# Layer two's feed-forward part: fifteen taps of a third tile on VectorE, joined on TensorE by an identity; means subtracted from PSUM; the residual projection at the head of a strip's tail

## The chip, the cores and the metric

The kernel runs on one core of one Trainium2 chip. The metric is the device time of one execution in microseconds, the median of several runs. A profiled execution is a separate one, and its own time is given beside them.

## The reference, cut to what matters

The network has four layers over four images of 64x64 tokens with 96 channels. The selective scans of the first two take the first 12030 us of the profile's 15132. The change touches only the feed-forward part of the second layer. Its input `y` has 192 channels, it works on 768 hidden channels (`HID`), and it ends in 96:

```python
def msffn(y, in_w, in_b, dw1, dw3, dw5, ln_g, ln_b, out_w, out_b):
    hcl = jax.nn.silu(y @ in_w.T + in_b)
    hc = hcl.transpose(0, 3, 1, 2)
    hc = hc + dwconv(hc, dw1) + dwconv(hc, dw3) + dwconv(hc, dw5)
    hn = layernorm(hc.transpose(0, 2, 3, 1), ln_g, ln_b)
    return hn @ out_w.T + out_b
```

`dwconv` is a convolution with one filter per channel over the 64x64 image. The three of them and the identity are folded into one 5x5 filter of 25 taps. Beside this the layer adds the projection of `y` to 96 channels and the residual `x`, with a skip factor.

## The kernel before

The 768 hidden channels are six tiles of 128 partitions, numbered 0 to 5. The tokens are eight strips of 32 image rows (2048 tokens, four chunks of 512). For one strip and one tile the kernel

- zeroes a padded image `pad` of 36x68 on GpSimd (L1657), makes the hidden values with TensorE into PSUM tile `c` (L1666; four pieces of 512 tokens and a remainder of 128, two halves of the 192 channels each), and writes silu of it into `pad` on ScalarE (L1674). Tiles `ON_PE = (0, 2, 3, 5)` use `padp` (two buffers), tiles 1 and 4 use `padv` (one buffer);
- convolves. For the tiles on TensorE (`on_pe`), each tap is 16 matmuls with a diagonal 32x32 weight, at 16 positions of the array (L1697), added up in four PSUM banks `d0` to `d3`, of which there is one set. ScalarE copies them out in 16 pieces into `hcp` (L1712). For tiles 1 and 4 (`on_dve`) VectorE does one multiply (L1731) and 24 multiply-adds (L1733) over the whole strip, in `hcv`.

When a strip's six tiles are there, `leave` ends the strip, which is called its tail here: TensorE adds the channels up into the mean (`average`, L1743; the four chunks at the four column positions of the array), ScalarE copies it out (L1765), TensorE spreads it over the partitions chunk by chunk (L1770), ScalarE copies that to `means` (L1774), VectorE subtracts it from each of the six tiles (L1778), ScalarE squares them (L1750, a thread of its own, at most two ahead), TensorE averages the squares (L1743), ScalarE and VectorE make the reciprocal deviation (L1793, L1795). Then, for each chunk: spread it (L1799), copy it (L1809), project `y` (L1814), add to the residual `x` (L1818), six output matmuls (L1823), two VectorE operations (L1825, L1827), and a store (L1828). PSUM tile `m`, used for everything that is spread, projected or put out, has one buffer. The residual `x` is loaded at L1783, in the middle of the tail.

Each engine runs its instructions in the order in which they were issued. That order is set by the class `Plan`. Every step of work is a Python generator (a thread: `loads`, `leave`, `enter` for either group of tiles, `on_pe`, `on_dve`). It names an engine and a duration (`yield "PE", 5.3`) before it issues, or a condition that it waits for. `Plan.run` keeps a time for every engine, always takes the thread that could start soonest, and after each step lets it go on 0.2 us later. So the durations written in the code decide how threads are interleaved. `loads` issues a strip's `y` load (L1642, 1632 KB) once the strip two before it is `done`, as its buffer is one of two.

Of the kernel before, what the change touches and what calls it, by code (L numbers as in the profile page):

```python
# [211 lines left out]
class Plan:  # L212
# [3 lines left out]
    def __init__(self, fill=None):  # L216
        self.threads, self.free, self.fill, self.current = [], {}, fill, None
# [20 lines left out]
    def run(self):  # L238
        now = 0.0
        while self.threads:  # L240
# [20 lines left out]
            th.wants = next(th.work, None)  # L261
            if th.wants is None:
                self.threads.remove(th)
# [1310 lines left out]
def layer1_ffn(k, a, x_in, y_in, x_out):  # L1574
# [5 lines left out]
    with ExitStack() as ctx:  # L1580
# [23 lines left out]
        ON_PE = (0, 2, 3, 5)  # L1604
        taps = k.load(w, a["L1_dw5"], "taps")
# [26 lines left out]
        plan, held = Plan(), {"c": 0}  # L1632
        for st in strips:
            st.lo, st.hi = max(0, st.r0 - 2), min(HW, st.r0 + ROWS + 2)
            st.y, st.pads, st.hc, st.ready, st.done = None, {}, {}, set(), False
        old = lambda st, n: st.n < n or strips[st.n - n].done

        def loads():
            for st in strips:
                yield lambda: old(st, 2)  # L1640
                st.y = k.t(io, [C, 2, (ROWS + 4) * HW], "y")
                nc.sync.dma_start(  # L1642
                    st.y[:, :, : (st.hi - st.lo) * HW],
                    y_in[:, st.b, st.lo * HW : st.hi * HW].rearrange("(h c) t -> c h t", c=C),
                )
                yield "DMA", 10.0
# [36 lines left out]
        def on_pe():  # L1683
            for st in strips:
                for t in ON_PE:
                    yield lambda: st.pads.get(t) is not None
                    pad = st.pads[t]

                    pc = [k.t(psd, [128, CH], f"d{i}") for i in range(4)]
                    for tap in range(25):  # L1690
                        if tap % 5 == 0:
                            yield "PE", 5.3
                        dy, dx = divmod(tap, 5)
                        for i in range(4):
                            mine = slice(i * 32, (i + 1) * 32)
                            for j in range(4):
                                nc.tensor.matmul(  # L1697
                                    pc[i][j * 32 : (j + 1) * 32, :],
                                    diag[mine, ON_PE.index(t), tap, :],
                                    pad[mine, j * 8 + dy : j * 8 + dy + 8, dx : dx + HW],  # L1700
                                    start=tap == 0,
                                    stop=tap == 24,
# [4 lines left out]
                    yield lambda: st.n == 0 or ON_PE.index(t) < 2 or strips[st.n - 1].done  # L1707
                    hc = k.t(io, [128, ROWS * HW], "hcp", bufs=6)
# [8 lines left out]

        def on_dve():
            for st in strips:
                for t in ON_DVE:  # L1720
                    yield lambda: st.pads.get(t) is not None
                    pad = st.pads[t]
                    yield lambda: st.n == 0 or t == ON_DVE[0] or strips[st.n - 1].done
                    hc = k.t(io, [128, ROWS * HW], "hcv", bufs=3)
                    to = hc.rearrange("p (r w) -> p r w", w=HW)
                    for tap in range(25):
                        yield "DVE", 2.35
                        dy, dx = divmod(tap, 5)
                        win, wt = pad[:, dy : dy + ROWS, dx : dx + HW], taps[:, t, tap : tap + 1]
                        if tap == 0:  # L1730
                            nc.vector.tensor_scalar_mul(to, win, wt)  # L1731
                        else:
                            nc.vector.scalar_tensor_tensor(to, win, wt, to, op0=ALU.mult, op1=ALU.add)  # L1733
# [7 lines left out]
        def average(ps, v, first, last):  # L1741
            for at, cols in chunks:
                nc.tensor.matmul(ps[at, :], avg, v[:, cols], start=first, stop=last, tile_position=(0, at.start))  # L1743

        def squares(st):
            for t in st.order:
                yield lambda: t in st.centred and len(st.squared) - st.summed < 2
                sq = k.t(work, [128, ROWS * HW], "sq", bufs=2)
                yield "ACT", 1.9
                nc.scalar.activation(sq, st.hc[t], AF.Square)  # L1750
                st.squared.append(sq)

        def leave():
            for st in strips:
                st.order, st.centred, st.squared, st.summed = [], set(), [], 0
                mean = k.t(psm, [128, CH], "s")
                while len(st.order) < NT:
# [3 lines left out]
                    yield "PE", 1.0  # L1761
# [4 lines left out]
                means = k.t(work, [128, ROWS * HW], "means", bufs=1)  # L1766
                for at, cols in chunks:
# [5 lines left out]
                    yield "ACT", 0.6  # L1773
                    nc.scalar.copy(means[:, cols], p)  # L1774
                plan.add(squares(st))
                for t in st.order:
                    yield "DVE", 2.3
                    nc.vector.tensor_sub(st.hc[t], st.hc[t], means)  # L1778
                    st.centred.add(t)
                xs = []  # L1780
                for at, cols in chunks:
                    x = k.t(work, [C, CH], "x", bufs=4)
                    nc.sync.dma_start(x, x_in[:, st.b, st.r0 * HW + cols.start : st.r0 * HW + cols.stop])  # L1783
                    xs.append(x)
                var = k.t(psm, [128, CH], "s")
                for n in range(NT):
                    yield lambda: len(st.squared) > n
                    yield "PE", 1.0
                    average(var, st.squared[n], n == 0, n == NT - 1)
# [6 lines left out]
                for j, (quarter, cols) in enumerate(chunks):  # L1796
# [13 lines left out]
                    pp = k.t(ps, [C, CH], "m")  # L1810
                    at = (st.r0 - st.lo) * HW + j * CH
                    yield "PE", 1.8
                    for half in range(2):
                        nc.tensor.matmul(  # L1814
# [664 lines left out]
```

## Time and profile before

| what | us |
|---|---|
| runs, median of 3 | 15260.64 (15258.76 to 15286.69) |
| profiled execution, its own time | 15133.75 |
| span of the profile | 15131.9 |
| the stage: first c matmul, end of strip 0, end of strip 6, last VectorE operation | 12049.8, 12422.8, 13813.6, 13965.8 |
| one strip in the middle, from y load to y load | 231.5 to 232.0 |

The span runs from the first to the last instruction of the execution. A line of the groups reads: line, engine, operation, output and input by the program's names, shapes, count | busy time, mean ns of one | idle time of the engine ahead of them and what ended it. A line of the waits reads: who <- whom: us in total, times, longest. A line of a timeline reads: start, duration, engine, line, operation, names, shapes, count of records, and the idle time ahead in brackets; a matmul of 32-bit numbers shows as two records. "The granted clock" is the share of TensorE's full clock that the chip let through.

### The profile page before, as it was taken

To read this page: it belongs to the slowest core of one execution; us is meant where nothing else is said; L and a number is where in the kernel's file an instruction comes from. 1 tells how busy PE (TensorE), PEld (TensorE's weight loads), DVE (VectorE), ACT (ScalarE), POOL (GpSimd) and SP (SyncE) were. 2 spreads that over 40 slices of the span, in tenths; PEclk is the share of its full clock that TensorE was granted. 3 is DMA by queue.
4 is the path that set the end of the run, shared out by engine and by line. 5 is a ranking of instruction groups with operands and counts; after the bars stand their busy time and mean duration, and the time that the engine had idled before them with its cause. 6 is when DMAs were issued, how large, how long until landed. Compare 5 with 4: busy or idle time off the path is not lost. (4 is left out here: it accounts for less than half of the span.)

```text
span 15131.9 us, 190905 instructions
## 1 busy us (share of the span) xinstructions
PE 13534.7 (89%) x71561; PEld 4825.7 (32%) x71561; DVE 12601.9 (83%) x9389; ACT 8242.6 (54%) x13165; POOL 9773.6 (65%) x4913
## 2 busy tenths in 40 slices
PE   8899899989998999899989998998899889898877
PEld 3232323232323232322222223222222244443344
DVE  1999799979997999799979997999999855565655
ACT  3666466656665666466656665665566333332333
POOL 0788688868886888688858885887788600000123
PEclk9899899989998999899989998999899899998888
DMA  2333433343334333445455445445545400000122
GB/s 69 120 122 118 160 115 124 117 156 124 115 126 147 126 113 127 160 158 165 159 164 167 160 149 177 162 151 163 174 156 165 140 11 12 18 19 17 48 72 71
DMA packets 713945, 1821.70 MB, mean 120 GB/s; under 512 B 108966, under 2 KB 274603, under 8 KB 709244
## 3 DMA queue, kind: packets, MB, share of 16 engines
q1 hardware_dynamic: 676156, 1733.94, 35.5%
q0 software_dynamic: 36864, 75.55, 1.7%
q8 instruction: 566, 9.27, 0.3%
q14 instruction: 359, 2.94, 0.1%
HBM read 1429.25 MB, written 379.91 MB: 120 GB/s over the span
## 5 line engine op out<-in xcount | busy, mean ns | idle before, releaser
L1155 POOL TENSOR_TENSOR hc<-h,bc 128x1024 f32<-128x1024 f32 x2304 | 5413.4, 2364 | 769.7 <-DVE h L1135 706.0
L1135 DVE TENSOR_TENSOR_SCAN h<-da,state,t 128x1024 f32<-128x1024 f32 x2112 | 4836.4, 2327 | 3.1 <-ACT da L1124 3.1
L1128 DVE TENSOR_TENSOR t<-u,bc 128x1024 f32<-128x1024 f32 x2816 | 3309.2, 1216 | 280.1 <-PE u L1116 198.5
L1124 ACT ACTIVATE da<-dts,L_A_logs 128x1024 f32<-128x1024 f32 x2816 | 3188.1, 1146 | 597.0 <-DVE h L1135 562.6
L1164 PE MATMUL y<-hc,gather_y 128*32 128x512 f32 x9216 | 2807.7, 643 | 44.7 <-POOL hc L1155 44.5
L1155 POOL TENSOR_TENSOR area<-h,bc 128x1024 f32<-128x1024 f32 x768 | 1813.8, 2362 | 652.7 <-DVE h L1135 593.8
L1116 PE MATMUL u<-dtu,spread 32*128 32x512 f32 x3072 | 1705.9, 679 | 416.4 <-DVE t L1128 406.8
L1135 DVE TENSOR_TENSOR_SCAN h<-da,t 128x1024 f32<-128x1024 f32 x704 | 1569.8, 2266 | 16.7 <-ACT da L1124 8.8
L1182 PE MATMUL y<-L_diag,zeros 96*32 96x256 f32 x5024 | 1263.0, 388 | 0.0
L1050 ACT COPY dt<-m 96x512 f32<-96x512 f32 x512 | 297.2, 580 | 1355.2 <-PE m L1047 1354.5
L1164 PE MATMUL y<-area,gather_y 128*32 128x512 f32 x3072 | 1005.1, 739 | 5.1 <-ACT yc L1193 3.6
L1116 PEld LDWEIGHTS u<-dtu,spread 32*128 32x128 f32 x3072 | 546.2, 197 | 1405.3 <-issue 948.7
L1164 PEld LDWEIGHTS y<-hc,gather_y 128*32 128x32 f32 x9216 | 523.6, 115 | 1379.6 <-issue 953.0
L1657 POOL MEMSET padp<- 128x2448 f32 x32 | 68.4, 2139 | 1385.8 <-PE d L1697 1368.3
L1733 DVE SCALAR_TENSOR_TENSOR hcv<-padv,taps,hcv 128x2048 f32<-128x2048 f32 x384 | 902.2, 2349 | 13.4
L1697 PE MATMUL d<-padp,diag 32*32 32x512 f32 x25600 | 885.7, 601 | 2.0 <-ACT hcp L1712 2.0
L1182 PEld LDWEIGHTS y<-L_diag,zeros 96*32 96x32 f32 x5024 | 522.6, 112 | 811.9 <-issue 458.3
L1107 POOL TENSOR_TENSOR area<-area,bc 128x1024 f32<-128x1024 f32 x256 | 603.3, 2357 | 172.7 <-DMA area<-u_dram 172.7
L963 PE MATMUL m<-xs,proj 96*128 96x512 f32 (+1 forms) x1024 | 553.2, 649 | 86.8 <-ACT spare L1209 39.7
L963 PE MATMUL m<-area,proj 96*128 96x512 f32 (+1 forms) x1024 | 549.9, 648 | 88.7 <-ACT dt L978 41.0
L1047 PE MATMUL m<-dtu,ident 96*96 96x512 f32 x1024 | 582.8, 652 | 24.9 <-ACT xs L937 12.4
L1697 PEld LDWEIGHTS d<-padp,diag 32*32 32x32 f32 x25600 | 482.7, 103 | 371.4 <-issue 196.9
(289 smaller groups left out, 18174.1 us busy)
## 6 DMA issues: line engine op xcount, KB each, us to landing
bc<-bc_dram SPq DMA_DIRECT2D x1024, 512.0 KB
dts<-dt_dram SPq DMA_DIRECT2D x768, 512.0 KB
area<-u_dram SPq DMA_DIRECT2D x256, 512.0 KB
dt_dram<-dt SPq DMA_DIRECT2D x256, 384.0 KB
y_tok<-spare SPq DMA_DIRECT2D x64, 768.0 KB
dt<-y_tok SPq DMA_DIRECT2D x128, 384.0 KB
u_dram<-dtu SPq DMA_DIRECT2D x128, 384.0 KB
x_tok<-area SPq DMA_DIRECT2D x32, 768.0 KB
```

Of the source, the lines that this page charges most:

```text
L963: nc.tensor.matmul(v.ps, seg.proj[:, src, to], seg.xs[:, src, chunks[j]], start=src == 0, stop=src == 1)
L1047: nc.tensor.matmul(v.ps, k.ident[:C, :C], term[:, half, chunks[j]], start=at == 0, stop=at == 3)
L1107: self.nc.gpsimd.tensor_mul(gr.t, gr.u, self.bc[:, 0, gr.sg, :])
L1116: self.nc.tensor.matmul(seg.u[:, cols], self.spread[rows, :], seg.dtu[rows, half, cols], start=True, stop=True)
L1124: self.nc.scalar.activation(gr.da, gr.seg.dts[gr.cb], AF.Exp, scale=scale)
L1128: self.nc.vector.tensor_mul(gr.t, gr.seg.u, self.bc[:, 0, gr.sg, :])
L1135: self.nc.vector.tensor_tensor_scan(gr.h[:, order], gr.da[:, order], gr.t[:, order], start, op0=ALU.mult, op1=ALU.add)
L1155: self.nc.gpsimd.tensor_mul(gr.hc, gr.h, self.bc[:, 1, gr.sg, :])
L1164: nc.tensor.matmul(seg.y[at : at + GC, :], self.gather_y, gr.hc[:, part * CH : (part + 1) * CH], start=gr.sg == 0, stop=gr.sg == NSG - 1, ...
L1182: self.nc.tensor.matmul(gr.seg.y[at : at + GC, :256], self.zeros, gr.seg.bt.lay.diag.rearrange("p h t c -> p (h t c)")[:, :256], start=Fal ...
L1697: nc.tensor.matmul(pc[i][j * 32 : (j + 1) * 32, :], diag[mine, ON_PE.index(t), tap, :], pad[mine, j * 8 + dy : j * 8 + dy + 8, dx : dx + H ...
L1733: nc.vector.scalar_tensor_tensor(to, win, wt, to, op0=ALU.mult, op1=ALU.add)
```

## The change

- Tile 3 (`SHARED`) is convolved by two engines: TensorE does its taps 0 to 9 (`ROWS_PE = 2` rows of five), VectorE does taps 10 to 24 into the tile's own `hcp` buffer, and TensorE adds that buffer to the four PSUM banks by 16 matmuls with a 32x32 identity. VectorE takes the tiles in the order 1, 3, 4.
- The spread mean isn't copied to `means`: VectorE subtracts it from PSUM, chunk by chunk (24 operations in place of six). The squares and their averages go in two halves of 1024 tokens.
- The load of `x`, the four projections of `y` and the adding to `x` come first in `leave`, before the means.
- `padp` has three buffers instead of two, `hcp` seven instead of six; `Plan(tight=True)` leaves the 0.2 us out when a thread's next step is on the same engine; some of the durations named in the code change. The threads `leave` and `squares` get precedence at equal times, and the buffer of `y` is two rows smaller (the loads are as they were).

```diff
             th.at = start + us + (0.2 if us else 0.0)
             th.wants = next(th.work, None)
+            if self.tight and isinstance(th.wants, tuple) and th.wants[0] == engine:
+                th.at -= 0.2
...
         ON_PE = (0, 2, 3, 5)
+        SHARED, ROWS_PE = ON_PE[2], 2
...
-        plan, held = Plan(), {"c": 0}
+        plan, held = Plan(tight=True), {"c": 0}
...
-                st.y = k.t(io, [C, 2, (ROWS + 4) * HW], "y")
+                st.y = k.t(io, [C, 2, (ROWS + 2) * HW], "y")
...
+                    hc = None
+                    if t == SHARED:
+                        hc = st.share = k.t(io, [128, ROWS * HW], "hcp", bufs=7)
+                    last = ROWS_PE * 5 if t == SHARED else 24
                     pc = [k.t(psd, [128, CH], f"d{i}") for i in range(4)]
-                    for tap in range(25):
-                        if tap % 5 == 0:
-                            yield "PE", 5.3
+                    for tap in range(last + 1):
+                        if tap % 5 == 0 and tap < 25:
+                            if t == SHARED and tap == last:
+                                yield lambda: st.shared
+                                yield "PE", 1.1
+                            else:
+                                yield "PE", 5.3
                         dy, dx = divmod(tap, 5)
                         for i in range(4):
                             mine = slice(i * 32, (i + 1) * 32)
                             for j in range(4):
+                                whole = t == SHARED and tap == last
                                 nc.tensor.matmul(
                                     pc[i][j * 32 : (j + 1) * 32, :],
-                                    diag[mine, ON_PE.index(t), tap, :],
-                                    pad[mine, j * 8 + dy : j * 8 + dy + 8, dx : dx + HW],
+                                    eye[mine, :] if whole else diag[mine, ON_PE.index(t), tap, :],
+                                    hc[mine, j * CH : (j + 1) * CH]
+                                    if whole
+                                    else pad[mine, j * 8 + dy : j * 8 + dy + 8, dx : dx + HW],
                                     start=tap == 0,
-                                    stop=tap == 24,
+                                    stop=tap == last,
...
-                    yield lambda: st.n == 0 or ON_PE.index(t) < 2 or strips[st.n - 1].done
-                    hc = k.t(io, [128, ROWS * HW], "hcp", bufs=6)
+                    if hc is None:
+                        yield lambda: st.n == 0 or t in ON_PE[:2] or strips[st.n - 1].done
+                        hc = k.t(io, [128, ROWS * HW], "hcp", bufs=7)
...
+        def convolve(pad, t, hc, first):
+            to = hc.rearrange("p (r w) -> p r w", w=HW)
+            for tap in range(first, 25):
+                yield "DVE", 1.3 if tap == first else 2.35
+                dy, dx = divmod(tap, 5)
+                win, wt = pad[:, dy : dy + ROWS, dx : dx + HW], taps[:, t, tap : tap + 1]
+                if tap == first:
+                    nc.vector.tensor_scalar_mul(to, win, wt)
+                else:
+                    nc.vector.scalar_tensor_tensor(to, win, wt, to, op0=ALU.mult, op1=ALU.add)
+
         def on_dve():
             for st in strips:
-                for t in ON_DVE:
+                for t in (ON_DVE[0], SHARED, ON_DVE[1]):
+                    if t == SHARED:
+                        yield lambda: st.share is not None
+                        yield from convolve(st.pads[t], t, st.share, ROWS_PE * 5)
+                        st.shared = True
+                        continue
...
                     yield lambda: st.n == 0 or t == ON_DVE[0] or strips[st.n - 1].done
                     hc = k.t(io, [128, ROWS * HW], "hcv", bufs=3)
-                    to = hc.rearrange("p (r w) -> p r w", w=HW)
-                    for tap in range(25):
...
+                    yield from convolve(st.pads[t], t, hc, 0)
                     st.pads[t] = None
...
+        def average(ps, v, first, last, part=chunks):
+            start = part[0][1].start
+            for at, cols in part:
+                mine = v[:, cols.start - start : cols.stop - start]
+                nc.tensor.matmul(ps[at, :], avg, mine, start=first, stop=last, tile_position=(0, at.start))
...
         def squares(st):
-            for t in st.order:
-                yield lambda: t in st.centred and len(st.squared) - st.summed < 2
-                sq = k.t(work, [128, ROWS * HW], "sq", bufs=2)
-                yield "ACT", 1.9
...
+            for half in range(2):
+                for t in st.order:
+                    yield lambda: st.centred > half and len(st.squared) - st.summed < 2
+                    sq = k.t(work, [128, ROWS * HW // 2], "sq", bufs=2)
+                    yield "ACT", 1.05
+                    nc.scalar.activation(sq, st.hc[t][:, half * 2 * CH : (half + 1) * 2 * CH], AF.Square)
+                    st.squared.append(sq)
...
         def leave():
             for st in strips:
-                st.order, st.centred, st.squared, st.summed = [], set(), [], 0
-                mean = k.t(psm, [128, CH], "s")
+                st.order, st.centred, st.squared, st.summed = [], 0, [], 0
+                mean, xs = k.t(psm, [128, CH], "s"), []
+                yield lambda: st.y is not None
+                for at, cols in chunks:
+                    x = k.t(work, [C, CH], "x", bufs=4)
+                    nc.sync.dma_start(x, x_in[:, st.b, st.r0 * HW + cols.start : st.r0 * HW + cols.stop])
+                    xs.append(x)
+                for j in range(4):
+                    pp = k.t(ps, [C, CH], "m")
+                    at = (st.r0 - st.lo) * HW + j * CH
+                    yield "PE", 1.8
+                    for half in range(2):
+                        nc.tensor.matmul(
+                            pp, proj_w[:, half, :], st.y[:, half, at : at + CH], start=half == 0, stop=half == 1
+                        )
+                    yield "DVE", 0.75
+                    nc.vector.scalar_tensor_tensor(xs[j], xs[j], cb, pp, op0=ALU.add, op1=ALU.add)
                 while len(st.order) < NT:
                     yield lambda: st.ready - set(st.order)
                     t = min(st.ready - set(st.order))
                     st.order.append(t)
-                    yield "PE", 1.0
+                    yield "PE", 1.4
                     average(mean, st.hc[t], len(st.order) == 1, len(st.order) == NT)
                 yield "ACT", 0.6
...
-                means = k.t(work, [128, ROWS * HW], "means", bufs=1)
-                for at, cols in chunks:
+                plan.add(squares(st), 1)
+                for j, (at, cols) in enumerate(chunks):
                     yield "PE", 0.9
                     p = k.t(ps, [128, CH], "m")
                     nc.tensor.matmul(
...
-                    yield "ACT", 0.6
-                    nc.scalar.copy(means[:, cols], p)
-                plan.add(squares(st))
-                for t in st.order:
-                    yield "DVE", 2.3
-                    nc.vector.tensor_sub(st.hc[t], st.hc[t], means)
-                    st.centred.add(t)
-                xs = []
-                for at, cols in chunks:
-                    x = k.t(work, [C, CH], "x", bufs=4)
-                    nc.sync.dma_start(x, x_in[:, st.b, st.r0 * HW + cols.start : st.r0 * HW + cols.stop])
-                    xs.append(x)
+                    yield "DVE", 3.8
+                    for t in st.order:
+                        nc.vector.tensor_sub(st.hc[t][:, cols], st.hc[t][:, cols], p)
+                    st.centred = (j + 1) // 2
...
-                for n in range(NT):
+                for n in range(2 * NT):
                     yield lambda: len(st.squared) > n
-                    yield "PE", 1.0
-                    average(var, st.squared[n], n == 0, n == NT - 1)
+                    yield "PE", 0.7
+                    half, at = divmod(n, NT)
+                    average(var, st.squared[n], at == 0, at == NT - 1, chunks[2 * half : 2 * half + 2])
                     st.summed += 1
...
                     nc.scalar.copy(rs, p)
-                    pp = k.t(ps, [C, CH], "m")
...
-                    yield "DVE", 0.7
-                    nc.vector.scalar_tensor_tensor(xs[j], xs[j], cb, pp, op0=ALU.add, op1=ALU.add)
                     po = k.t(ps, [C, CH], "m")
...
-        plan.add(leave())
-        plan.add(enter(ON_PE, "padp", 2))
+        plan.add(leave(), 1)
+        plan.add(enter(ON_PE, "padp", 3))
```

## The prediction, made before the result was known

> **What bounds the kernel now.** I read the utilisation by slice first, for where the changed stage lies (12038 to 13966 us of the span of 15131.9), then one steady strip of it through the windows view, the groups, the waits and the timelines, and last the end of the stage.
>
> The windows view of a strip (us, then each engine's busy time, granted clock, DMA share, GB/s):
>
> ```profile
> 12666.40:12897.90 231.50, 212.23 (x3496) 95.74 (x3496) 140.05 (x69) 74.69 (x112) 12.83 (x6) 0.96 0.07 16
> ```
>
> TensorE is busy 212 of 231.5 us, VectorE 140, ScalarE 75: TensorE bounds the strip, and VectorE has about 90 us of room. Six such periods, 231.8 each, lie between the end of strip 0 and the end of strip 6. The groups of the strip (busy, mean ns | idle before, releaser) and its waits:
>
> ```profile
> L1733 DVE SCALAR_TENSOR_TENSOR hcv<-padv,taps,hcv 128x2048 f32<-128x2048 f32 x48 | 112.8, 2349 | 1.7
> L1697 PE MATMUL d<-padp,diag 32*32 32x512 f32 x3200 | 111.0, 600 | 0.0
> L1778 DVE TENSOR_TENSOR hcp<-hcp,means 128x2048 f32<-128x2048 f32 x4 | 9.0, 2285 | 45.4 <-ACT means L1774 45.4
> L1825 DVE TENSOR_TENSOR rs<-rs,m 96x512 f32<-96x512 f32 x4 | 2.7, 684 | 21.8 <-PE m L1823 21.8
> ```
> ```profile
> PE c L1666 <- DMA y<-y: 12.5, 1, 12.5
> PE s L1743 <- ACT hcp L1712: 6.2, 2, 4.4
> ```
>
> The taps are over half of TensorE's work. Its idle time is 19.4 us: 12.5 for the y load, 6.2 for ScalarE's copies out of PSUM, 0.8 small. The timeline shows prices and what follows a wait:
>
> ```profile
> 12666.47 3.75 PE L1666 MATMUL c<-y,in_w 96*128 96x512 f32 x4 [12.48 <-DMA y<-y]
> ...
> 12672.35 1.98 PE L1666 MATMUL c<-y,in_w 96*128 96x512 f32 x4
> ...
> 12681.75 5.55 PE L1697 MATMUL d<-padp,diag 32*32 32x512 f32 x160
> ...
> 12721.27 3.72 PE L1743 MATMUL s<-hcp,avg 128*32 128x512 f32 x8 [4.43 <-ACT hcp L1712]
> ...
> 12783.98 1.06 PE L1743 MATMUL s<-sq,avg 128*32 128x512 f32 x8
> ```
>
> Start to start, five taps cost 5.49, a c pair 1.91 (0.64 for the 2-row remainder), an averaging call 1.0, a row spread 1.04, a projection 1.8, six output matmuls 5.2. The strip is then 20x5.49 + 24x1.91 + 6x0.64 + 12x1.0 + 8x1.04 + 4x1.8 + 4x5.2 = 208; with 19.4 idle 227; the other 4 are the slow instructions behind a wait (3.75 for 1.98, 3.72 for 1.06).
>
> **The change on TensorE, by strip.** Tile 3 keeps 10 of its 25 taps: three groups of five go, -16.5. The identity adds 16 matmuls of the taps' own shape, 16/80 of a group: +1.1. The averages of squares become 12 calls with two column positions instead of 6 with four. No row shows such a call. Two passes of one position follow each other, and a whole-width pass takes 1.91/4 = 0.48, so two positions cost 0.96, as much as four do now; if the price went by count it would be 0.5. I take 1.0, +6 (bounds 0 and +6). Work: 208 - 16.5 + 1.1 + 6 = 198.6.
>
> **VectorE, by strip.** The shared tile adds one multiply (1.28) and 14 taps at a pitch of 2.39 (24 take 57.33): +34.8. The subtractions become 24 of 128x512 with one operand in PSUM; the nearest row with such an operand is L1825, 0.684, the SBUF form's share is 2285/4 = 571, so 13.7 to 16.4 against 13.7 now. Busy about 177 of some 219: still not the bound by sum. The Trainium skill ("VectorE: DVE Perf Modes", Rules for kernel authors) advises a copy out of PSUM where many operations read a matmul's output, which speaks against this edit; by the rows it is worth 2.7 us on VectorE, against four copies (2.3) dropped from ScalarE. Since the PSUM tile m has one buffer, the spread of chunk n+1 waits for six subtractions (about 4 us); between two spreads TensorE has a c pair and five taps (7.4), which cover it. If that cover went, it would cost 4 us three times.
>
> **ScalarE, GpSimd, SyncE.** Six squares of 1.91 become twelve, each between 0.69 (512 wide) and 1.91, about 1.09: +1.6, minus the four mean copies. The third padp buffer moves a 2.14 us memset ahead; at the start GpSimd waits 5.2 us for eye anyway, so it is free there. On SyncE's queue four x loads per strip still follow the y load, but are now wanted at once.
>
> **Waits on TensorE after it,** in the changed program's order of instructions:
> - y load. It is still issued after the last store of the strip before. From the last output matmul to the first c was 12.4 us with nothing between; now a c remainder, five taps and the first projection (0.64 + 5.49 + 1.8 = 7.9) stand there: 4.5 left.
> - x loads. y and x ended together 12.2 us after the last o (DMA share 0.91 until 12668, then 0.03). VectorE's first x add now waits for that, some 5 us, with the last four shared taps and all 25 taps of tile 4 queued behind it.
> - identity. Counting from that o: x add done 12.9, two taps 17.7, x add 18.4, two taps 23.2. TensorE: c pair 12.9, projection 14.7, two pairs 18.5, projection 20.3, pair 22.2. It waits about 1. Until then the four PSUM banks of the taps are held, so tile 5 can't start.
> - tile 5's copies: five taps' end to the average as now, 4.4 idle and 2.7 of stretching; the like wait of 1.7 before it now has c pairs over it. 7.1.
> - tile 4's average: VectorE is done at 23.2 + 0.7 + 3.7 + 0.7 + 55 = 83.3; TensorE gets there at 24.3 + 1.8 + 55.7 = 81.8 (taps 27, seven c pairs and two remainders 14.7, five averages 5, that wait 7.1, one more pair 1.9). Wait 2.
> - squares: only two may be ahead of TensorE. ScalarE needs 12x1.09 + four copy groups of 2.35 + four activations of 0.7 = 25; TensorE has 12 + 5.5 + 4x1.91 + 1.3 = 26 in that stretch. They alternate; I take 4 (0 to 10).
> - half clock behind the y wait: 1.8 as now.
>
> Sum 4.5 + 1 + 7.1 + 2 + 4 + 1.8 = 20.4; the period becomes 219, 13 less. Six periods: -77. The first has 16 groups for 17 (-5.5), two c pairs more (+3.8), and of the cover of the y load only a pair (+6): +4.
>
> **Head and tail.** Up to the end of strip 0 (373 us now): six groups of taps less (-32.9), identity 1.1, two c pairs and a remainder less (-4.5), squares +6, new waits some +8: -22. The tail now:
>
> ```profile
> 13813.61 1.06 PE L1743 MATMUL s<-hcp,avg 128*32 128x512 f32 x8
> ...
> 13873.88 1.94 PE L1743 MATMUL s<-hcv,avg 128*32 128x512 f32 x8 [17.41 <-DVE hcv L1733]
> ...
> 13910.93 3.73 PE L1814 MATMUL m<-y,proj_w 96*96 96x512 f32 x4 [0.67 <-ACT rs L1809]
> ```
>
> The last strip ends on VectorE: it runs tile 4 from 13815 to 13874, and 152 us pass from strip 6's end to strip 7's. After the change it must first add x and finish the shared taps, about 20 later. The second half of the squares starts after the last subtraction: +8. Four projections leave the output rounds (2.6 + 0.84 each): -14. Together +14.
>
> -77 + 4 - 22 + 14 = -81. The profiled execution took 15133.75 (span plus 2); the median of the runs is 127 us above it (0.8%), spread over no stage I can see, and I carry the saving over unscaled: 15260.6 - 81 = 15180.
>
> **The rivals.**
> 1. Half clock at every wait. The granted clock was 0.50 from 12660 to 12668, in and behind the y wait, and a c group took 3.75 for 1.98; behind 4.43 idle an average took 3.72 against 2.85 behind 1.73. One wait of 12 becomes several of 2 to 7; if each slows what follows by some 1.8, two or three per strip add 4 to 5.5, a period of 224, and the gain is about 50: 15210. Against it: waits of 1.7 and less had no such cost. The Trainium skill ("TensorE: Matmul & The Clock Gate", Part 1) has the clock halve after an idle window of about 3.4 us, which agrees with these rows.
> 2. Slower: the shared tile holds the PSUM banks. If VectorE reaches its 15 taps late, TensorE stands at the identity with nothing of tile 5 allowed. Each microsecond of lateness costs one per strip, and from about 13 per strip nothing is gained. With 20 more than now counted, a period of 239: +45 over six, with head and tail +35, 15300. For it: 6 shared taps stand behind the third output round on VectorE, and the x loads land late. Against: four output rounds and projections space both engines alike, and my count has them within 1 us.
> 3. The waits are simply exchanged: squares at 10, copies at 10, y load hardly shorter (the gain of the projections going to waiting for x). Period 229: -25, 15235.
> 4. Larger gain: half-size averages at 0.5 and the squares' wait at 0, period 209: -140, 15120.
>
> **How the numbers follow.** Forecast (gain 60 to 110) 0.55; rival 1 0.15; rival 3 0.09; rival 2 0.08; rival 4 0.13. The range 15125 to 15240 takes in the forecast, rival 1 and most of 3 and 4. 0.2% is 30 us, about what a measurement here tells from no change (the three runs span 28). Faster by more: 0.55 + 0.15 + 0.13 and a little of rival 3, 0.85; within 0.07; slower 0.08.
>
> **What would show it.** Right: a strip period near 219 in the windows, taps at 17 groups, TensorE's wait for the y load at 4 to 5, about 2 at tile 4's average, VectorE at 175 to 180 busy. Wrong: a wait of TensorE for VectorE's hcp (identity) of over 5, averages of squares at 0.5, VectorE busy throughout, or a period over 228.

## The result, and the profile after

The changed kernel took 15153.8 us (median of 6 runs, 15146.18 to 15185.33), the kernel before 15261.31 (6 runs, 15258.11 to 15286.69): a ratio of 0.9931, 95% interval 0.9918 to 0.9944, or 86 to 125 us. The forecast was 15180, a gain of 81.

The profiled execution of the changed kernel took 15172.17 us, 38 more than that of before (15133.75), though the kernel is faster. The difference lies ahead of the changed stage: the stage's first matmul (a projection now, a c matmul before) came at 12201.7 us of the span, against 12049.8, behind code that the change doesn't touch. So the ruler here is the stage alone, from the start of its first matmul to the start of its last VectorE operation: 1915.3 us before, 1797.0 after, 118 less. What follows it took 1166.8 and 1171.4.

A steady strip of the changed kernel, windows view (us, then the busy time of TensorE, weight loads, VectorE, ScalarE, GpSimd; granted clock, DMA share, GB/s):

```profile
12980.10:13195.00 214.90, 200.80 (x3050) 88.69 (x3049) 175.14 (x103) 73.75 (x114) 14.45 (x6) 0.97 0.07 17
```

The period fell from 231.5 to 214.9. TensorE's work fell by 11.4 and its waits by 5.2 (14.1 for 19.3); VectorE does 35 us more and still has 40 to spare. The groups of that strip (busy, mean ns | idle before, releaser):

```profile
L1743 DVE SCALAR_TENSOR_TENSOR hcv<-padv,taps,hcv 128x2048 f32<-128x2048 f32 x48 | 112.8, 2350 | 1.7
L1710 PE MATMUL d<-padp,diag 32*32 32x512 f32 x2720 | 92.8, 600 | 0.0
L1743 DVE SCALAR_TENSOR_TENSOR hcp<-padp,taps,hcp 128x2048 f32<-128x2048 f32 x15 | 35.2, 2349 | 0.4
L1816 DVE TENSOR_TENSOR hcp<-hcp,m 128x512 f32<-128x512 f32 x16 | 10.3, 683 | 17.0 <-PE m L1811 17.0
L1850 DVE TENSOR_TENSOR rs<-rs,m 96x512 f32<-96x512 f32 x4 | 2.7, 682 | 6.8 <-PE m L1848 6.8
```

The first two lines stood at 112.8 and 111.0: VectorE's own tiles cost the same, TensorE has 2720 tap matmuls for 3200, and VectorE's extra taps are the third line. An operation with one operand in PSUM costs 683 ns, as the output's did (last line). TensorE's waits in the strip:

```profile
PE c L1670 <- DMA y<-y: 4.8, 1, 4.8
PE s L1768 <- ACT hcp L1728: 4.4, 1, 4.4
PE s L1768 <- ACT sq L1776: 3.9, 7, 0.6
```

The wait for y was 12.5. There is none at the identity in any strip but the last (3.23 there). The timeline of the next strip's start shows why:

```profile
13193.99 1.02 PE L1848 MATMUL m<-hcv,out_wg 128*96 128x512 f32 x2
13194.85 0.61 PE L1670 MATMUL c<-y,in_w 96*128 96x128 f32 x4
13195.39 5.56 PE L1710 MATMUL d<-padp,diag 32*32 32x512 f32 x160
13200.88 1.96 PE L1793 MATMUL m<-y,proj_w 96*96 96x512 f32 x4
13207.79 3.75 PE L1670 MATMUL c<-y,in_w 96*128 96x512 f32 x4 [4.96 <-DMA y<-y]
...
13220.32 1.14 PE L1710 MATMUL d<-hcp,eye 32*32 32x512 f32 x32
...
13235.81 26.06 PE L1710 MATMUL d<-padp,diag 32*32 32x512 f32 x800
...
13271.66 3.72 PE L1768 MATMUL s<-hcp,avg 128*32 128x512 f32 x8 [4.44 <-ACT hcp L1728]
...
13279.04 1.06 PE L1768 MATMUL s<-hcv,avg 128*32 128x512 f32 x8 [1.03 <-DVE hcv L1743]
...
13327.85 1.05 PE L1768 MATMUL s<-sq,avg 128*32 128x512 f32 x4 [0.65 <-ACT sq L1776]
```

From the end of the last output matmul (first line) to the c matmul that waits for y pass 12.8 us, 12.5 before; but a remainder of c, a group of five taps and a projection (the next three lines) now stand in that time. The identity has no wait in brackets. The last line is the half-size averaging call: two positions of the array cost 1.05 where four cost 1.06 (the line above it).

### The profile page after: what moved, and what is told of

Read it like the earlier page. It is cut to its first block, busy times and chain, and to the rows that moved or that the text cites. A ratio compares the mean times of both kernels' runs of the same rounds, so it can differ in the third digit from the quotient of the medians.

```text
span 15170.1 us, 184061 instructions
## 1 busy us (share of the span) xinstructions
PE 13616.5 (90%) x67977; PEld 4793.1 (32%) x67977; DVE 12867.4 (85%) x9653; ACT 8240.9 (54%) x13181; POOL 9741.4 (64%) x4913
## 4 chain that ended last, share of the span: by engine, by line
PE 53%; DVE 17%; issue 13%; ACT 11%; DMA 3%; POOL 1%; SPq 1%; ACTq 0%; DVEq 0%; POOLq 0%; another core or an unknown queue 0%
PE y L1166 12%; PE m L1049 10%; PE u L1118 7%; DVE h L1137 6%; DVE t L1130 5%; PE m L965 4%; PE d L1710 3%; PE y L1184 3%; DVE hcv L1743 3%; ACT da L1126 2%; PE t L569 2%; PE c L1670 1%; PE m L925 1%; ACT sp_z L1015 1%; PE m L1207 1%
## 5 line engine op out<-in xcount | busy, mean ns | idle before, releaser
L1710 PE MATMUL d<-padp,diag 32*32 32x512 f32 x21760 | 746.4, 602 | 0.0
L1058 POOL TENSOR_TENSOR dtu<-dt,xs 96x1024 f32<-96x1024 f32 x128 | 301.9, 2358 | 464.5 <-ACT dt L1052 464.0
```

Source lines behind the costliest of these rows:

```text
L1710: nc.tensor.matmul(pc[i][j * 32 : (j + 1) * 32, :], eye[mine, :] if whole else diag[mine, ON_PE.index(t), tap, :], hc[mine, j * CH : (j + ...
```

## The experiments

The theory: TensorE sets the strip, so the gain is the taps taken from it, as long as the order of instructions keeps work in front of the y load and VectorE's part of the shared tile is in time. The rivals: the waits would shrink without the moved taps; or the shared tile's late arrival eats the gain. The kernels of one set ran on one chip, beside the kernel before. "Period" is from one strip's reciprocal (L1829 in the changed kernel) to the next's, without the first and the last; "stage" is as above.

| kernel | period, us | stage, us | median, us | before, us | ratio, 95% interval |
|---|---|---|---|---|---|
| e1_noshare | 235.6 | 1909.8 | 15134.34 | 15149.57 | 0.9993 (0.9984 to 1.0003) |
| e2_tailsend | 227 to 240 | 1913.3 | 15144.38 | 15149.57 | 0.9997 (0.9988 to 1.0007) |
| e3_shareonly | 241 to 247 | 2001.2 | 15233.61 | 15149.57 | 1.0057 (1.0038 to 1.0076) |
| e5_changed | 215 to 216 | 1795.1 | 15131.88 | 15286.6 | 0.9897 (0.9875 to 0.9918) |
| e6_y_early | 208 to 216 | 1776.2 | 15130.93 | 15286.6 | 0.9902 (0.9881 to 0.9924) |
| e7_y_early_row1 | 227 to 229 | 1877.5 | 15231.2 | 15286.6 | 0.9966 (0.9951 to 0.9982) |
| e8_shared_last | 288 to 297 | 2411.1 | 15777.72 | 15286.6 | 1.0325 (1.0303 to 1.0347) |
| e9_padp2 | 216 to 225 | 1815.4 | 15203.44 | 15290.17 | 0.994 (0.9923 to 0.9957) |
| e10_whole_padp2 | 232.1 | 1886.0 | 15268.37 | 15290.17 | 0.9981 (0.997 to 0.9992) |
| e11_whole_y | 220 to 224 | 1825.1 | 15205.03 | 15290.17 | 0.9945 (0.9927 to 0.9962) |
| e12_means_padp2 | 215 to 222 | 1801.5 | 15042.08 | 15156.32 | 0.9933 (0.9917 to 0.995) |
| e13_loose | 238 to 239 | 1944.2 | 15172.48 | 15156.32 | 1.0011 (1.0001 to 1.002) |

### e1: without the shared tile

```diff
-        SHARED, ROWS_PE = ON_PE[2], 2
+        SHARED, ROWS_PE = None, 2
-                for t in (ON_DVE[0], SHARED, ON_DVE[1]):
+                for t in ON_DVE:
```

> The changed kernel with tile 3 wholly on TensorE again; means from PSUM, projections first, three padp buffers stay. Theory A (TensorE's work is what the strip's period is made of, and the moved taps are the gain): +16.5 - 1.1 us per strip, a period of 229 to 231, the stage 90 to 105 longer with a shorter last strip, about 15250. Rival B (the gain comes from the reordered tail, and the moved taps only swap places with waits): 15190 at the most, period under 221.

All of the gain is gone. TensorE was busy 216.5 of 235.6 us, 15.7 more than in the changed kernel (the prediction's 16.5 for three groups less 1.1 for the identity is 15.4); and it waits 19.1, 5 more. The start of a strip in its timeline:

```profile
13103.58 1.02 PE L1848 MATMUL m<-hcp,out_wg 128*96 128x512 f32 x2
13104.44 0.61 PE L1670 MATMUL c<-y,in_w 96*128 96x128 f32 x4
13116.81 3.75 PE L1670 MATMUL c<-y,in_w 96*128 96x512 f32 x4 [11.76 <-DMA y<-y]
```

In this order neither taps nor a projection stand behind the last outputs. So having the projections at the head of the tail doesn't by itself shorten the wait for y; the group of taps that covers it has that place in the changed kernel's order, and not in this one.

### e2: projections and x back in the output rounds

```diff
+                    pp = k.t(ps, [C, CH], "m")
+                    at = (st.r0 - st.lo) * HW + j * CH
+                    yield "PE", 1.8
...
+                    nc.vector.scalar_tensor_tensor(xs[j], xs[j], cb, pp, op0=ALU.add, op1=ALU.add)
                     po = k.t(ps, [C, CH], "m")
```

(The same lines go from the head of `leave`, with the loads of x.)

> The changed kernel with the x load, the projections and the x add back in the output rounds. Theory A: the wait for the y load is bare again (12.4 instead of 4.8) and the first add of x no longer stalls VectorE, so 6 to 8 us per strip more, and 14 in the last strip: 15200 to 15215. Rival B (the position of the projections does not matter, as the y load is issued at the same place): within 15 of the changed kernel.

Again the gain is gone, 19 us per strip on average, more than twice what I had expected. The wait for y was 12.23 in the strip that I read and the c behind it took 3.75; output matmuls waited up to 2.9 for VectorE's x. Over two strips TensorE was busy 210.6 us each, 10 more than in the changed kernel, and waited 26 each, 12 more. I had counted the projections, and not that the order around them changes too.

### e3: the shared tile alone

The kernel before with the shared tile, two `padp` and six `hcp` buffers. With six `hcp` buffers the shared tile's has to wait for the strip before to be done:

```diff
+                    if t == SHARED:
+                        yield lambda: st.n == 0 or strips[st.n - 1].done
+                        hc = st.share = k.t(io, [128, ROWS * HW], "hcp", bufs=6)
```

> The kernel before with the shared tile alone: two padp and six hcp buffers, means copied to SBUF, whole squares, projections in the output rounds. Theory A: 15 less per strip of TensorE's work and the same waits as before, a period near 217 to 220, a last strip 20 to 30 longer: 15165 to 15195. Rival C (without the other edits VectorE is late at the identity and TensorE stands there): period over 226, 15230 or more.

Slower than before, and by the mechanism of the prediction's second rival. TensorE at the identity:

```profile
12933.07 2.02 PE L1709 MATMUL d<-hcp,eye 32*32 32x512 f32 x32 [16.86 <-DVE hcp L1742]
```

It waits 17 to 20 us per strip there (36.6 in two), against the 16.5 that the taps are worth. VectorE's rows show where the lateness comes from:

```profile
12897.64 0.75 DVE L1849 SCALAR_TENSOR_TENSOR o<-rs,skip,x 96x512 f32<-96x512 f32 x1
12898.31 1.28 DVE L1740 TENSOR_SCALAR hcp<-padp,taps 128x2048 f32<-128x2048 f32 x1
12899.62 33.39 DVE L1742 SCALAR_TENSOR_TENSOR hcp<-padp,taps,hcp 128x2048 f32<-128x2048 f32 x14
```

All fifteen shared taps stand behind the strip's last output operation (first line), where the added condition puts them, though VectorE had been idle for 23.7 us in the output rounds before it (6.93, 8.20, 3.03 and 5.55). In the changed kernel's strip nine of the fifteen are done by then. So e3 shows what a late join costs, and not what the shared tile would be worth by itself.

### e5, e6, e7: the y load earlier, and then more taps on VectorE

e5 is the changed kernel itself, for the comparison: stage 1795.1 where the first profile had 1797.0. e6 issues a strip's y load once the projections of the strip two before are issued, in place of behind its last store; e7 also leaves TensorE only five of the shared tile's taps.

```diff
-                yield lambda: old(st, 2)
+                yield lambda: st.n < 2 or strips[st.n - 2].projected
```
```diff
-        SHARED, ROWS_PE = ON_PE[2], 2
+        SHARED, ROWS_PE = ON_PE[2], 1
```

> The changed kernel itself beside the other variants, so that all stand against the same runs of the kernel before. All theories: the stage 118 us shorter than before, as its profile has it (1797 against 1915), so a ratio of 0.992 to 0.993.

> The changed kernel, but the y load of strip n is issued once the projections of strip n-2 are (its last reader), not when that strip is done. Theory A (the period is TensorE's work plus its waits): the y wait of 4.8, the half clock behind it (1.9) and VectorE's 7 us of waiting for x go: 6 to 7 us less per strip and 11 in the first, 45 less than the changed kernel. Rival B (VectorE's chain from the x add to tile 4's average paces the strip, so that waits only move): within 12 of the changed kernel.

> The same with one row of five taps of tile 3 on TensorE and 20 on VectorE. Theory A: TensorE -5.5 per strip, VectorE +12 to some 188 busy of 205: 10 to 40 less than with two rows if VectorE still has room. Rival B (VectorE's chain paces): TensorE stands at the identity or at tile 4's average, 6 to 12 more per strip, 30 to 90 more than with two rows.

e6's waits, two strips (us in total, times, longest):

```profile
PE s L1769 <- ACT hcp L1729: 14.5, 4, 4.4
PE s L1769 <- ACT sq L1777: 8.7, 10, 1.7
```

The wait for y is gone, and nearly all of that for x; but the period stays at 214.4 to 217 until the last strips (208 twice, then 186 where it was 181.5). The 5 us came back: the copies out of PSUM are waited for twice per strip (2.8 and 4.4), and small waits stand at x and the identity (1.8 and 1.0 in the two strips). The stage was 19 us shorter than e5's; the medians of four runs each are 1 us apart, so a gain over the changed kernel isn't shown.

e7 shows the room on VectorE. With five taps more it is busy 185.9 us of 228, and its bound is a time, not a sum:

```profile
13038.54 2.02 PE L1711 MATMUL d<-hcp,eye 32*32 32x512 f32 x32 [12.15 <-DVE hcp L1744]
```

TensorE has 5.5 us less to do and waits 12 more there, and more for x (8.5 in two strips, 1.8 in e6). So five taps on TensorE are too few; between that and ten lies the point where the two meet, and fifteen weren't tried.

### e8: the shared tile last on VectorE

```diff
-                for t in (ON_DVE[0], SHARED, ON_DVE[1]):
+                for t in (ON_DVE[0], ON_DVE[1], SHARED):
```

> The changed kernel with VectorE's tiles in the order 1, 4, 3, so that the shared taps come last and the identity late. Theory C (the PSUM banks held until the identity keep tile 5 from starting, so lateness costs one for one): a wait of TensorE for VectorE at the identity of 20 to 40 per strip, period 235 to 250, 130 to 270 more than the changed kernel. Rival (other work covers it): under 40 more.

The same instructions, 73 to 82 us more per strip. The waits of one strip:

```profile
PE s L1768 <- DVE hcv L1743: 38.1, 1, 38.1
PE d L1710 <- DVE hcp L1743: 24.1, 1, 24.1
```

In each strip the four banks wait 24 us for VectorE, with no tap of tile 5 to do meanwhile, and the average of tile 4 waits 38 us. In the strips of 297 us TensorE's work also grew, from 200.8 to 212.5 us, at a granted clock of 0.85 for 0.97; the three together are 74 of the 82.

### e4, e9, e10, e11: whole squares; two padp buffers

e4 was to be the changed kernel with whole squares, six averaging calls of 2048 tokens in place of twelve of 1024, and a period of 207 to 212 was expected. It has no time: with three `padp` buffers its pool would need 74.25 KB per partition where 67.78 are left. So whole squares could only be tried on top of two `padp` buffers, which e9 prices alone.

```diff
-        plan.add(enter(ON_PE, "padp", 3))
+        plan.add(enter(ON_PE, "padp", 2))
```

> The changed kernel with two padp buffers, as before the change, in place of three. The shared tile keeps its padded image until VectorE has read it for its 15 taps, where a tile on TensorE alone gives it back after its own 25, so with two buffers the c matmuls of the tile after next come later. Theory: nothing of the gain is in this buffer by itself, but the c pairs that fill TensorE's wait at the identity and behind the copies need it: the wait at the identity, 0 with three buffers, becomes 2 to 6, period 217 to 221 for 215, stage 1812 to 1845 for 1797, time 20 to 50 us longer than the changed kernel. Rival 1: the buffer does nothing, period 215, stage within 5 us of 1797. Rival 2: it carries the change: TensorE waits for silu into pad at every tile, period 228 or more, stage over 1900.

The expectation held in the stage, 18 us longer. But the period is 225 in the first strips and 216 later, and the place is another: the wait is not at the identity but at a projection, for x.

```profile
13012.33 2.02 PE L1793 MATMUL m<-y,proj_w 96*96 96x512 f32 x2 [8.41 <-DVE x L1797]
```

Since `m` has one buffer, the second projection waits until VectorE has added x to the first, and x lands behind y. In this order only c matmuls and a projection stand between the last outputs and that wait, and no group of taps.

e10 adds whole squares, e11 the early y load of e6:

```diff
-            for half in range(2):
-                for t in st.order:
-                    yield lambda: st.centred > half and len(st.squared) - st.summed < 2
-                    sq = k.t(work, [128, ROWS * HW // 2], "sq", bufs=2)
+            for t in st.order:
+                yield lambda: st.centred > 1 and len(st.squared) - st.summed < 2
+                sq = k.t(work, [128, ROWS * HW], "sq", bufs=2)
...
```

> As e9 (two padp buffers, which leaves the memory for it), with the squares and their averages whole, 2048 tokens and four column positions, six calls per strip, in place of two halves and twelve calls; the squares start when all four chunks are subtracted. If a call with two positions costs what one with four does (1.05 and 1.06 in the traces), TensorE's work falls by 6 us per strip, and its waits for the squares by some 2 of 3.9, but the first square starts about 8 us later. Theory: the 8 us lie under taps of the next strip, except at the end of the last strip: period 5 to 8 shorter than e9's, the stage 30 to 50 shorter, the last strip's end some 6 longer. Rival: with the halves gone TensorE's fillers no longer fit between the subtractions and the averages, and the wait for the first square comes to 4 to 8 per strip: period as e9's or longer.

> As e10, with a strip's y load issued once the projections of the strip two before it are issued (as e6), in place of behind its last store. Candidate to beat the changed kernel. Theory: TensorE's wait for y of about 5 us per strip goes, VectorE's wait for x too, and of the 5 some 2 to 3 come back as waits at the identity and at the squares: period 2 to 3 below e10's, stage 15 to 25 shorter than e10's and 40 to 60 shorter than the changed kernel's 1797, so about 1745. Rival: VectorE is the bound once TensorE's work falls below 195 per strip (VectorE works 175 and waits for its tiles' pads): the wait only moves to the identity, stage within 10 us of e10's.

For e10 the rival's outcome came, a period no shorter than e9's, but not for its reason, a longer wait for the squares. TensorE has six averaging calls less, but e10's period is 232.1, 7 to 16 longer than e9's. Its waits in 450 us, some two strips:

```profile
PE s L1768 <- ACT hcp L1728: 16.6, 4, 4.4
PE m L1792 <- DVE x L1796: 12.0, 2, 6.0
PE d L1710 <- DVE hcp L1743: 11.1, 2, 5.5
PE m L1846 <- ACT rs L1841: 5.7, 2, 2.8
```

Against the same stretch of e9, the waits for squares fell from 8.7 to 3.0 and those for x from 16.8 to 12.0, but the 11.1 at the identity and 5.7 at the outputs are new. And the work did not fall: TensorE was busy 396.6 of 450 us, which is 204.6 of a period, and 410.7 in e9, which is 205.6 of one of 225.3, at a granted clock of 0.93 in e10 and 0.95 in e9; that the six calls' saving went into matmuls slowed behind the new waits fits this, and isn't shown more closely. In e11 neither the theory's stage of about 1745 nor the rival's, within 10 us of e10's, came. The wait for x there is 0.5 a strip and that at the identity stays at 5: the stage is 61 us shorter than e10's, and 28 longer than the changed kernel's, so it isn't the better version that I had hoped for.

### e12: the mean copied out of PSUM again

e9 with a ScalarE copy to `means` and six whole subtractions (`means` takes the room of the third `padp`):

```diff
+                means = k.t(work, [128, ROWS * HW], "means", bufs=1)
...
-                    yield "DVE", 3.8
-                    for t in st.order:
-                        nc.vector.tensor_sub(st.hc[t][:, cols], st.hc[t][:, cols], p)
-                    st.centred = (j + 1) // 2
+                    yield "ACT", 0.6
+                    nc.scalar.copy(means[:, cols], p)
+                for t in st.order:
+                    yield "DVE", 2.3
+                    nc.vector.tensor_sub(st.hc[t], st.hc[t], means)
+                    st.centred.add(t)
```

> As e9 (two padp buffers, for the memory), with the spread mean copied to means by ScalarE again and subtracted from whole tiles (six operations of 2.285 in place of 24 of 0.68), each tile's squares, still in halves, following as soon as it is subtracted. VectorE saves 2.7 us per strip (16.4 - 13.7), ScalarE gets four copies of 0.58 more, and TensorE's spreads no longer wait for six subtractions each. Theory: since TensorE sets the strip and its waits at the spreads are 0, the subtraction from PSUM is worth nothing by itself: period within 3 us of e9's (216 to 225), stage within 20 us of its 1815. Rival: the squares come earlier or later by their other order, and the waits for them change by more than 4 per strip: stage over 1840 or under 1790.

The stage is 1801.5, 14 shorter than e9's, within the 20 expected. The six subtractions were busy 13.6 us (9.0 and 4.6), as before the change. Here too waits were exchanged: e9's 16.8 us for x in 450 us are gone, and 7.5 stand at the identity. So with two `padp` buffers subtracting from PSUM brings no time; what it frees is the memory of `means`, which the third `padp` uses.

### e13: the planner's 0.2 us

```diff
-        plan, held = Plan(tight=True), {"c": 0}
+        plan, held = Plan(), {"c": 0}
```

> The changed kernel with Plan() in place of Plan(tight=True): the planner's clock again adds 0.2 us to each step, so that the order on the engines differs while the instructions are the same. Theory: the planner's VectorE runs late by 0.2 for each of 64 taps, 13 us per strip, as it counts 2.35 + 0.2 for 2.39; it then puts the identity and tile 4's average later among TensorE's other work than VectorE is really done. The waits at both stay 0 to 2, and the period within 4 us of 215; stage 1790 to 1830. Rival: what the 0.2 puts behind the identity is the work that covers the y load or the squares, and their waits grow: period 220 or more, stage over 1840.

My theory here fell, and the rival held. The instructions are the same, only their order differs, and the stage is 147 us longer than the changed kernel's, 29 longer than the kernel before's:

```profile
12878.48 1.02 PE L1848 MATMUL m<-hcv,out_wg 128*96 128x512 f32 x2
12892.64 3.75 PE L1670 MATMUL c<-y,in_w 96*128 96x512 f32 x4 [13.14 <-DMA y<-y]
...
12909.75 3.21 PE L1793 MATMUL m<-y,proj_w 96*96 96x512 f32 x4 [2.42 <-DVE x L1797]
12916.06 2.02 PE L1710 MATMUL d<-hcp,eye 32*32 32x512 f32 x32 [3.10 <-DVE hcp L1743]
```

The group of taps is no longer in front of the y load, all 13 us of which are waited for, and x and the identity come late behind it. Of the strip's 238.9 us TensorE is busy 207.9 and waits 31.0, against 200.8 and 14.1: 17 more of waiting, and 7 more of work for the same matmuls, at a granted clock of 0.93 for 0.97.

## Why the prediction was right, step by step

- **TensorE bounds the strip; the taps taken from it are the gain.** Right, in that there is no gain without them: e1, the changed kernel without the shared tile, gives all of it back. They aren't enough: e2 and e13 keep the moved taps and lose the gain too.
- **Work 198.6, with slow instructions 203.1 busy.** Measured 200.8. The step that was off is the price of a group of taps: 5.49 from start to start holds for a group with other work behind it, but tile 5's 25 taps now run in a row and took 26.06, or 5.21 a group. 17 groups were busy 92.8 and 20 were 111.0, 18.2 less and not 16.5.
- **A half-width averaging call costs as much as a whole one, +6.** Right: 1.05 against 1.06. This ends rival 4, which needed 0.5. That twelve calls cost TensorE 6 us didn't make six calls better (e10).
- **The waits.** y load 4.5: 4.8. Identity 1: 0. Tile 5's copies 7.1: 4.44 idle, and 3.72 for a call of 1.06, 7.1 in all. Tile 4's average 2: 1.0. Squares 4: 3.9. Half clock behind y 1.8: 3.75 for 1.98. With the work this is the 4 us between a period of 219 and one of 215.
- **x behind y.** VectorE waited 7.0 for x (some 5 forecast), and still had the shared tile ready at 13219.2, 1.1 us before TensorE came to the identity. The prediction had VectorE later by 1; so close, a count of this kind can't tell a wait from none, and that none came was luck in part.
- **First period, head, tail.** From the end of strip 0 to that of strip 1 it took 221.0, 6 longer than the steady strips (4 forecast). (A strip ends with its last output matmul.) The head went from 373.1 to 341.9, -31 for -22. The tail went from 151.4 to 158.1, +7 for +14: VectorE started tile 4 some 19 us after the end of strip 6 (20 forecast), TensorE came to the tile's average 78 us after that end, 60 before; from there to the output rounds it took 41.6 for 34.4, +7 where 8 was forecast; and the four rounds took 38.2 for 56.8, -19 for -14. The price of 4 us for a spread that waits for six subtractions, which the steady strips don't pay, shows in this tail:

```profile
13918.81 1.93 PE L1768 MATMUL s<-hcv,avg 128*32 128x512 f32 x8 [8.47 <-DVE hcv L1743]
...
13927.29 2.07 PE L1811 MATMUL m<-mean,rows_of 32*128 32x512 f32 x2 [3.77 <-DVE hcv L1816]
```

- **The sum.** -94 for the six periods (-73 forecast), -31, +7: -118 where -81 was forecast. Of the 37 us between them 21 are the period's, 9 the head's, 7 the tail's.
- **Carried over unscaled.** The runs' 107.5 us lie between the two. That the gap between the profiled execution and the median lay outside the stage was assumed; the section below has what was seen of it.
- **Rival 1, half clock at every wait.** Two waits per strip had it, both in the sum already: behind 4.96 a c group took 3.75 for 1.98, behind 4.44 an average 3.72 for 1.06, both at a granted clock of 0.50. Behind 1.03 and less nothing was slower. The Trainium skill ("TensorE: Matmul & The Clock Gate", Part 1) has the clock go to half after an idle window of about 3.4 us; these rows agree, and e10's identity does (2.02 for 1.14 behind 5.54). e13's identity was as slow behind 3.10, with a wait of 2.42 shortly before it. But the prediction puts too much of the average's 2.7 us of stretching down to the clock. The average's four chunks wait, one after another, for ScalarE's last copies, which come 0.60 us apart (a weight load stands ahead of each chunk's matmuls):

```profile
13271.03 2.38 ACT L1728 COPY hcp<-d 32x512 f32<-32x512 f32 x4
13272.25 0.18 PEld L1768 LDWEIGHTS s<-hcp,avg 128*32 128x32 f32 x2 [0.42 <-ACT hcp L1728]
13272.86 0.18 PEld L1768 LDWEIGHTS s<-hcp,avg 128*32 128x32 f32 x2 [0.42 <-ACT hcp L1728]
```

  These three steps are 1.8 of the 2.7, and only 0.9 are left for the clock. The kernel before shows the 1.8 alone: its average of 2.85 behind 1.73, which the prediction names, ran at a granted clock of 1.00.
- **Rival 2, the shared tile holds the banks.** Not in the changed kernel's steady strips, but true as a mechanism: e3, e7 and e8 waited 17 to 20, 12 and 24 us per strip at the identity, and each was slower than the kernel without that lateness.
- **What the prediction didn't price.** It read the waits from the changed program's order, and had no term for how much hangs on that order. e13 shows that the 0.2 us of `Plan(tight=True)`, to which it gave no number, is worth more than the whole change.

## What to carry to other kernels

Work that moves to an idle engine pays only while that engine is in time where the two meet, so compare the instants at the meeting point and not the sums: five more taps on an engine with 40 us to spare cost 14 us per strip. What stands in front of an unhidden load is worth as much as the work removed, and it can hang on a planner's constant; after each edit, read the order around the longest wait again. Parts of such a change can't be valued one by one, since each removal reorders the rest: three single removals each lost the entire gain.

## What the runs showed of the hardware that was not expected

- **The time of the scans differs by 110 to 170 us with nothing changed in them.** The first matmul of the changed stage came between 12054.7 and 12061.7 us in all five kernels of the two sets on one chip (before: 15149.57 and 15156.32 there), and between 12171.3 and 12226.0 in the seven on two other chips (before: 15286.6 and 15290.17), where it also differs by 41 and 27 us among the kernels of one chip. The profile of before (12049.8) is of the first kind; its timed runs, at 15260, look like the second, of which no profile of before was taken. That would account for the 127 us that the prediction saw between them. The cause stays open. It is as large as the change, and medians taken on one chip aren't quite free of it: e5 gains 155 us by its medians and 120 by its stage. No kernel's stage was taken on both kinds of chip; the unchanged part behind the stage took 1159 to 1174 us in every profile.
- **Two of four column positions cost as much as four:** 1.05 and 1.06 us for a call with 512 columns of 32-bit numbers.
- **An operand in PSUM cost VectorE nothing that the rows show; cutting an operation in four did.** A 128x512 subtraction from PSUM took 0.683 us and a quarter of the 2048-wide one 0.571. But in the same strip a 96x512 operation with one operand in PSUM (the add to x, L1797) took 0.740, and one with all of them in SBUF, the on-chip memory (the output, L1852), 0.748, where a quarter of a 2048-wide tap is 0.587. The 2.7 us per strip that the prediction gives for the subtractions are thus those of 24 short operations in place of six long ones, and nothing in the strip noticed them.
